# First batch row by token tiles with zero matmuls in the waits, spikes in two rows, additions in turn: a spike and mixture-of-experts layer on one core

## The chip, the core and the metric

The kernel runs on one core of a Trainium2 chip. The core has five engines with queues of their own: TensorE (PE, matmuls and transposes into PSUM; its weight loads are listed as PEld), VectorE (DVE), ScalarE (ACT), GpSimd (POOL) and SyncE (SP, which here only issues DMAs; ACT and POOL issue some too). Each engine takes its instructions in the order of its queue, and waits for others through semaphores. The metric is the device time of one execution in microseconds (us). Lines such as L536 are lines of the kernel before.

## The reference

The input `x` is 16 rows of 256 tokens with 256 features, `cond` is 16 x 256, all float32. Two layers are each added to their input:

```python
# layer 0: spikes
rates = relu(x) * 0.001
c = cond[:, None, :] + cumsum(rates, axis=1)          # along the tokens
spikes = floor(c) - previous token's floor(c)         # floor(cond) ahead of token 0
x = x + spikes / 0.001
# layer 1: one shared expert and 2 of 8 routed experts
shared = (silu(x @ w1) * (x @ w3)) @ w2               # 256 -> 512 -> 256
s = sigmoid(concat(x, cond) @ router_W)               # 8 scores for each token
top 2 of s + router_bias; gates = their s, divided by their sum
routed = sum over the 2 of gate * gelu(x @ W1e[e]) @ W2e[e]   # 256 -> 256 -> 256
x = x + (shared + routed) / 3
```

## The kernel before

**Chunks.** The 4096 tokens are cut into 8 chunks of 512, that is two batch rows each. A chunk's `x` is loaded token by partition (`xn`), turned by PE (`turn`, L275) so that features lie on partitions and tokens along the free axis, and goes through the spikes:

- `rate` (ACT, L282) makes relu(x) * 0.001, `keep_x` (ACT, L291) keeps the turned x.
- `scan` (DVE, L306) is a running sum that starts again every 16 tokens (the tile `keep` holds 1, and 0 at each start); `sums` (L316 to L321) copies the last value of each stretch into `tot`, scans those, and adds the result to the stretches.
- `start` (ACT, L334) adds `cond` as a bias, `whole` (ACT, L343) converts to whole numbers, `floor` (DVE, L358 and L359) corrects rounding upwards, `spikes` (L370) subtracts the previous token's floor, `add` (L378) makes x1 = 1000 * spikes + x. The first column of `fl`, the floor of `cond`, is a small copy (L348).

The pieces of work are called `(first row, end, first feature half, end)`. Chunks 1 to 7 do each step on the whole chunk, 128 x 1024 elements (`elementwise`); chunk 0 does its first batch row in two halves by features, then its second row.

**Routing** (`route`): `pl` are the logits (L426), `lt` and `pn` turn them, `ex` is ACT's exp (L442); then some thirteen small DVE operations (L444 to L470) find the first and the second choice and give `hot`, which PE counts per expert (`pr`, L475 to L480). PE turns x1 back (`px`, L496), the place of each copy of a token is worked out (L502 to L509, `at_i`), and POOL scatters the rows to a list per expert in DRAM, `xs` (L513).

**Shared expert.** `shared_hidden` multiplies by w1 and w3 into three PSUM banks `ph` (L536), ACT takes Silu (L546), DVE the product `hs` (L547). `shared_out` multiplies by w2 into two PSUM banks `acc` (L563), DVE adds a third of it to x1 (L574). `all_shared` is one long generator of these pieces, and `unit(n)` takes n of them (1 is one of a chunk's four hidden parts, or half its output) at the place where it is called: this is how PE is kept at work beside everything else.

**Routed experts.** The weights of all experts lie in `we`, loaded in quarters (`load_experts`). `run_blocks` goes through up to 71 blocks of 128 rows of one expert: load from `xs`, DVE transposes, two matmuls (L859, L881) with Gelu between, scatter to `ys` (L890).

**End.** `combine` loads the two results of each token from `ys` in 16 pairs of 128-token tiles (`fetch`) and adds them, times the gate, to what is there (L996, four additions to a pair); a tile's last part to be done starts its store (L589). Pairs and the last shared units alternate.

**What sets the order.** Python emits one stream. Inside `tc.manual_schedule(engines=...)` the named engines keep the order as written; this holds for the start (L614 to L662: PE, ACT, DVE), for everything from the last chunk's routing through the blocks (L710), and for DVE at the end (L1007). Elsewhere, in the loop over chunks above all, a planner orders each queue by its own costs among what is ready, earlier text first; it may also move later work forward into gaps of a written order. SP and POOL are planned everywhere. All of it is fixed when the kernel is built.

Of the kernel before, what the change touches and what calls it, by code (L numbers as in the profile page):

```python
# [13 lines left out]
F32 = mybir.dt.float32  # L14
BF16 = mybir.dt.bfloat16
I32 = mybir.dt.int32
# [22 lines left out]
def kernel(  # L39
# [71 lines left out]
    def load_x(i, pieces=1):  # L111
        xn = xin.tile([P, J, D], F32, tag="xn", name=f"xn_{i}")
        src = xf[ts(i, N), :].rearrange("(j p) d -> p j d", p=P)
        for h in range(pieces):
            js = ts(h, J // pieces)
            nc.sync.dma_start(out=xn[:, js], in_=src[:, js])
        return xn


    xns = {0: load_x(0, NB)}  # L120
    cond_n = const.tile([B, D], F32)
    nc.scalar.dma_start(out=cond_n, in_=cond)
    rw = const.tile([P, 2 * KD, 32], F32)
    nc.vector.memset(rw, 0.0)
    nc.scalar.dma_start(
        out=rw[:, :, :E], in_=router_w.rearrange("(k p) e -> p k e", p=P)
    )
    rb = const.tile([P, E], F32)
    nc.scalar.dma_start(out=rb, in_=router_b.partition_broadcast(P))
# [5 lines left out]
    xns[1] = load_x(1)  # L135
    nc.sync.dma_start(out=w2_sb, in_=w2.rearrange("(s p) d -> p s d", p=P))
# [4 lines left out]
    def load_experts(g):  # L141

        for k in range(KD):
            nc.sync.dma_start(
                out=we_v[ts(g, Q), :, k],
                in_=w1e[:, (g * KD + k) * Q :][:, :Q, :].rearrange("e f h -> f e h"),
            )
        es = ts(g, 2)
        for k in range(KH):
            nc.sync.dma_start(  # L150
                out=we_v[:, es, KD + k], in_=w2e[es, ts(k, P), :].rearrange("e p d -> p e d")
            )
# [7 lines left out]
    keep = const.tile([P, KD * N], F32)  # L160
# [51 lines left out]
    def turn_cond():  # L212
        pc = p_t.tile([P, KD, B], F32, tag="pt", name="pc")
        for k in range(KD):
            nc.tensor.transpose(pc[:, k, :], cond_n[:, ts(k, P)], ident[:B, :B])
        nc.scalar.copy(cond_t, pc)
# [3 lines left out]
    def cond_floor():  # L220
        whole = const.tile([P, KD, B], I32, name="whole")
        nc.gpsimd.tensor_copy(whole, cond_t)
        nc.vector.tensor_tensor(cond_fl, whole, cond_t, ALU.is_gt)
        nc.vector.tensor_tensor(cond_fl, whole, cond_fl, ALU.subtract)
# [18 lines left out]
    class Spikes:  # L243
# [5 lines left out]

        def __init__(self, i):  # L250
            def tile(tag, dt=F32, last=T, pool=tmp):
                return pool.tile([P, NB, KD, last], dt, tag=tag, name=f"{tag}_{i}")

            self.i, self.tile, self.xn = i, tile, xns.pop(i)
            self.xt = prep.tile([P, KD, N], F32, tag="xt", name=f"xt_{i}")
            self.rates = tile("rates")

        @staticmethod
        def cut(t, part):

            b, bb, k, kk = part
            if bb - b == 1:
                return t[:, b, k:kk, :].rearrange("p k t -> p (k t)")
            return t[:, b:bb, k:kk, :].rearrange("p b k t -> p (b k t)")
# [32 lines left out]
        def scan_tiles(self):  # L297
            self.seg = self.tile("tb")
            self.tot, self.base = self.tile("tot", last=NSEG), self.tile("base", last=NSEG)
            self.cs, self.ri = self.tile("ta"), self.tile("tc", I32)  # L300
            nc.vector.memset(self.tot[:, :, :, 0:1], 0.0)

        def scan(self, part):

            seg = self.cut(self.seg, part)
            nc.vector.tensor_tensor_scan(  # L306
                seg, keep[:, : seg.shape[1]], self.cut(self.rates, part), 0.0, ALU.mult, ALU.add
            )

        def sums(self, part):  # L310

            seg, tot, base, cs = (
                self.cut(t, part) for t in (self.seg, self.tot, self.base, self.cs)
            )
            n = tot.shape[1]
            nc.vector.tensor_copy(  # L316
                tot.rearrange("p (g s) -> p g s", s=NSEG)[:, :, 1:],
                seg.rearrange("p (g s q) -> p g s q", s=NSEG, q=SEG)[:, :, : NSEG - 1, SEG - 1],
            )
            nc.vector.tensor_tensor_scan(base, keep[:, :n], tot, 0.0, ALU.mult, ALU.add)  # L320
            nc.vector.tensor_tensor(  # L321
                cs.rearrange("p (s q) -> p s q", q=SEG),
                seg.rearrange("p (s q) -> p s q", q=SEG),
                base[:, :, None].to_broadcast([P, n, SEG]),
                ALU.add,
            )
# [18 lines left out]
        def floor_tiles(self, pool=tmp, tag="tb", eng=nc.vector):  # L345

            self.fl = self.tile(tag, last=W, pool=pool)
            eng.tensor_copy(  # L348
                self.fl[:, :, :, 0].rearrange("p b k -> p k b"), cond_fl[:, :, ts(self.i, NB)]
            )  # L350
            self.x1 = x1s[self.i] = keepp.tile(
                [P, KD, N], F32, tag="x1", name=f"x1_{self.i}", bufs=6
            )

        def floor(self, part):

            up, ri = self.cut(self.cs, part), self.cut(self.ri, part)
            nc.vector.tensor_tensor(up, ri, up, ALU.is_gt)  # L358
            nc.vector.tensor_tensor(  # L359
                self.cut(self.fl, part).rearrange("p (g t) -> p g t", t=W)[:, :, 1:],  # L360
                ri.rearrange("p (g t) -> p g t", t=T),
                up.rearrange("p (g t) -> p g t", t=T),
                ALU.subtract,
            )
# [16 lines left out]

    def elementwise(i, sp=None):

        if sp is None:
            sp = Spikes(i)
            for k in range(KD):
                half = (0, NB, k, k + 1)
                pt = sp.turn(half)
                sp.rate(half, pt)
                sp.keep_x(half, pt)  # L390
            sp.next_load()
            yield
        part = (0, NB, 0, KD)
        sp.scan_tiles()
        sp.scan(part)
        yield
        sp.sums(part)
        yield
        sp.start(part)
        sp.whole(part)  # L400
        yield
        sp.floor_tiles()
        sp.floor(part)
        yield
        sp.spikes(part)
        yield
        sp.add(part)
        yield
# [4 lines left out]
    def route(i):  # L413
        x1, x1t = x1s[i], x1ts[i]

        def small(tag, shape=(P, J, E), dt=F32):
            return rt.tile(list(shape), dt, tag=tag, name=f"{tag}_{i}")
# [47 lines left out]
        )  # L465
        sel2 = small("sel2")
# [37 lines left out]
        at = small("at", (P, TOPK, J))  # L504
        for q in range(TOPK):
            nc.vector.tensor_tensor(mine[:, q], row, hots[q], ALU.mult)
        nc.vector.tensor_reduce(at, mine, AX.X, ALU.add)
        at_i = small("at_i", (P, TOPK, J), I32)
        placed[i] = nc.vector.tensor_copy(at_i, at)  # L509
# [84 lines left out]
    def all_shared():  # L594

        for i in range(NCHUNK):
            yield from shared_hidden(i, [slice(0, T), slice(T, N)] if i == 0 else [slice(0, N)])
            if i > 0:
                yield from shared_out(i - 1)
        yield from shared_out(NCHUNK - 1)  # L600
# [12 lines left out]

    with tc.manual_schedule(engines={PE, ACT, DVE}):  # L614
        sp = Spikes(0)
        halves = [(0, 1, k, k + 1) for k in range(KD)]
        row = (1, 2, 0, KD)
        pts = [sp.turn(part) for part in halves]
        for part, pt in zip(halves, pts):
            sp.rate(part, pt)  # L620
        turn_cond()
        for part, pt in zip(halves, pts):
            sp.keep_x(part, pt)
        sp.scan_tiles()
        for part in halves:
            sp.scan(part)
            sp.sums(part)
            sp.start(part)
            sp.whole(part)
        cond_floor()  # L630
        sp.floor_tiles(pool=hid, tag="ht", eng=nc.gpsimd)
        pt = sp.turn(row)
        sp.rate(row, pt)
        sp.keep_x(row, pt)
        sp.next_load()
        for part in halves:
            sp.floor(part)
            sp.spikes(part)
            sp.add(part)
        unit(0.5, whole=False)  # L640
        sp.scan(row)
        sp.sums(row)
        unit(0.5, whole=False)
        sp.start(row)
        unit(0.5, whole=False)
# [7 lines left out]
        unit(0.5, whole=False)  # L653
# [18 lines left out]
    next(ro)  # L672
    unit(0.5)
    next(ro)
    next(ro)
    next(ro)
    next(ro)
    next(el)
    unit(0.5)
    next(el)  # L680
# [4 lines left out]
    for i in range(2, NCHUNK):  # L685
# [9 lines left out]
        next(ro)  # L695
        unit()
# [6 lines left out]
        next(el, None)  # L703
# [10 lines left out]
    unit(0.5)  # L714
    next(ro)
# [270 lines left out]
    def combine():  # L986
        for n in range(SLOTS):
            fetch(n)
        for n, (i, h) in enumerate(pairs):
            yc = ycs.pop(n)  # L990
            for j in range(2):
                t = i * J + 2 * h + j
                last = x1ts[i][:, 2 * h + j, :, :FQ]
                for q in range(TOPK):
                    y = yc[:, j, TOPK - 1 - q]
                    nc.vector.scalar_tensor_tensor(  # L996
                        y, y, gates[:, q, t : t + 1], last, ALU.mult, ALU.add
                    )
                    last = y
# [55 lines left out]
```

## Time and profile before

| | |
|---|---|
| median of 3 runs | 337.07 us (336.89 to 337.3) |
| profiled execution | 337.38 us, of which the span of the core's instructions is 335.7 |
| PE busy in the span | 317.2 us (94%) |
| DVE, ACT, POOL busy | 231.5, 137.9, 165.6 us |
| first matmul of the shared expert | at 10.21 us |
| PE waits for `hot` between 46 and 132 us | 2.9 us in 5 times |
| blocks of routed experts end, last stage begins | about 285.4 us |
| DMA | 50.34 MB, mean 150 GB/s, 364 to 408 GB/s in the slices from about 293 to 319 us |

All times in the text count from the start of the span. A group's line gives its source line, engine and operation, output and inputs, shape and count, then busy time and the mean of one in ns. In a timeline a line begins with start and length in us, and in brackets the engine's idle time before it with what ended it. A wait's line gives who waited for whom, us in total, times, and the longest. Matmuls overlap, so a PE that is shown as busy can be slower than it could be: starts one after another tell the pace.

### The profile page before, as it was taken

Reading aid. Unit: us, or ns where it says so; the run is one execution under the profiler, and the core shown is the slowest. Engines: PE = TensorE matmul, PEld = TensorE weight load, DVE = VectorE, ACT = ScalarE, POOL = GpSimd, SP = SyncE. Lnnn points to the kernel's source line nnn. Section 1 sums busy time; section 2 is a strip of 40 time slices with the busy share of each in tenths; the row PEclk is TensorE's granted clock in tenths of the full one; section 3 lists DMA queues with packets and bytes.
Section 4 is the critical chain, followed back from the end, with each engine's and each line's share of the span. In section 5 each row is a group of like instructions: output and inputs, shape, how many; then the busy total and the mean of one; then the engine's idle time right before and its main releaser. Section 6 shows DMA issues by size and latency. Waiting matters only on the chain. (4 is left out here: it accounts for less than half of the span.)

```text
span 335.7 us, 6544 instructions
## 1 busy us (share of the span) xinstructions
PE 317.2 (94%) x1674; PEld 233.9 (70%) x1674; DVE 231.5 (69%) x656; ACT 137.9 (41%) x287; POOL 165.6 (49%) x197
## 2 busy tenths in 40 slices
PE   3799998999989999999999999999999999999985
PEld 2587644547546745746699998999999998474574
DVE  4677979999999996652467655555546551299993
ACT  4547385644675372040244443444444434201100
POOL 7000274787478687662045555555555565123220
PEclk9999999999999999999999999999999999999999
DMA  6999533242222112354456665765666662499913
GB/s 174 255 217 215 146 114 98 88 136 100 79 81 99 65 64 86 109 194 102 73 109 149 155 149 142 165 140 126 156 150 151 157 146 80 164 364 408 397 70 125
DMA packets 62534, 50.34 MB, mean 150 GB/s; under 512 B 42607, under 2 KB 52864, under 8 KB 62497
## 3 DMA queue, kind: packets, MB, share of 16 engines
q1 hardware_dynamic: 42240, 26.19, 32.0%
q0 software_dynamic: 7456, 20.86, 17.0%
q10 hardware_dynamic: 12800, 2.88, 5.0%
q8 instruction: 14, 0.23, 0.3%
q14 instruction: 24, 0.19, 0.2%
HBM read 27.44 MB, written 22.84 MB: 150 GB/s over the span
## 5 line engine op out<-in xcount | busy, mean ns | idle before, releaser
L536 PE MATMUL ph<-x,w_sb 128*128 128x512 f32 (+1 forms) x288 | 119.3, 561 | 4.9 <-DVE x L378 4.2
L890 POOL DMA_INDIRECT ys<-yb,to x67 | 66.2, 988 | 67.0 <-ACT yb L889 56.4
L513 POOL DMA_INDIRECT xs<-x1t,at_i x64 | 78.8, 1232 | 38.8 <-ACT xt L291 18.7
L536 PEld LDWEIGHTS ph<-x,w_sb 128*128 128x128 f32 x288 | 54.2, 196 | 53.5 <-issue 42.0
L859 PEld LDWEIGHTS phe<-xbt,w1e 128*128 128x128 f32 x536 | 70.3, 191 | 4.7 <-ACT hbt L867 0.9
L859 PE MATMUL phe<-xbt,w1e 128*128 128x128 f32 x536 | 70.7, 275 | 0.7 <-DVE xbt L832 0.7
L881 PE MATMUL py<-we,hbt 128*128 x268 | 68.9, 380 | 0.2 <-ACT hbt L867 0.2
L827 DVE COPY w1e<-we 128x512 f32 x67 | 29.1, 435 | 45.3 <-PE phe L859 43.8
L563 PE MATMUL pa<-w_sb,hs 128*128 128x256 f32 x256 | 58.2, 381 | 1.4 <-DVE x1t L574 1.1
L563 PEld LDWEIGHTS pa<-w_sb,hs 128*128 128x128 f32 x256 | 48.0, 190 | 11.1 <-issue 2.8
L881 PEld LDWEIGHTS py<-we,hbt 128*128 128x128 f32 x268 | 45.9, 191 | 3.9 <-ACT hbt L867 0.4
L546 ACT ACTIVATE as<-ph 128x512 f32<-128x512 f32 (+1 forms) x36 | 19.9, 553 | 64.5 <-PE ph L536 51.8
L867 ACT ACTIVATE hbt<-phe 128x256 f32<-128x256 f32 x67 | 25.8, 384 | 45.6 <-PE phe L859 35.2
L547 DVE TENSOR_TENSOR hs<-as,ph 128x512 f32<-128x512 f32 (+1 forms) x36 | 22.4, 623 | 27.5 <-PE ph L536 20.8
L889 ACT COPY yb<-py 128x256 f32<-128x256 f32 x67 | 24.9, 372 | 22.7 <-PE py L881 22.2
L832 DVE STREAM_TRANSPOSE xbt<-xb 128x256 f32<-128x256 f32 x67 | 29.3, 437 | 0.0
L306 DVE TENSOR_TENSOR_SCAN tb<-keep,rates 128x1024 f32<-128x1024 f32 (+2 forms) x10 | 18.8, 1876 | 1.4 <-ACT rates L282 1.3
L497 ACT COPY x1t<-px 128x512 f32<-128x512 f32 x16 | 8.6, 592 | 25.1 <-PE px L496 25.1
L589 POOL DMA_DIRECT2D out_dram<-yc x8 | 5.8, 729 | 23.9 <-DVE yc L996 22.1
L334 ACT ACTIVATE ta<-ta,cond_t 128x256 f32<-128x256 f32 x32 | 14.1, 498 | 8.1 <-DVE ta L321 7.1
L463 POOL COPY x1t<-first 128x16 f32<-128x16 f32 x8 | 4.2, 519 | 23.1 <-DVE first L456 23.1
L574 DVE SCALAR_TENSOR_TENSOR x1t<-pa,x1t 128x512 f32<-128x512 f32 x14 | 9.6, 684 | 6.3 <-PE pa L563 6.3
(135 smaller groups left out, 268.2 us busy)
## 6 DMA issues: line engine op xcount, KB each, us to landing
xb<-xs SPq DMA_DIRECT2D x184, 33.0 KB
yc<-ys SPq DMA_DIRECT2D x8, 512.0 KB
we<-ys SPq DMA_DIRECT2D x8, 512.0 KB
xn<-in_x_dram SPq DMA_DIRECT2D x7, 512.0 KB
xb<-xs ACTq DMA_DIRECT2D x84, 33.0 KB
we<-in_L_cond_W1e_dram SPq DMA_DIRECT2D x8, 256.0 KB
we<-in_L_cond_W2e_dram SPq DMA_DIRECT2D x8, 256.0 KB
out_dram<-yc POOLq DMA_DIRECT2D x8, 256.0 KB, 4.3
```

The source lines that it names most:

```text
L513: nc.gpsimd.indirect_dma_start(out=xs_w[(i * J + j) * TOPK + q][:, :], out_offset=bass.IndirectOffsetOnAxis(ap=at_i[:, q, j : j + 1], axis=0),
L536: nc.tensor.matmul(ph, lhsT=w[:, k, ts(u, P)], rhs=x1[:, k, cols], start=(k == 0), stop=(k == KD - 1),)
L546: nc.scalar.activation(act, ps[0], AF.Silu)
L547: nc.vector.tensor_tensor(ht[:, u, cols], act, ps[1], ALU.mult)
L563: nc.tensor.matmul(pa[:, q, :], lhsT=ht[:, s, ts(n * h + q, P)], rhs=w2_sb[:, s, :], start=(s == 0), stop=(s == KS - 1),)
L827: nc.vector.tensor_copy(w, we[:, bass.ds(off, KD * HE)])
L832: nc.vector.transpose(xt.rearrange("p g k r -> p g (k r)"), block[b].pop("xb")[:, :, :FQ])
L859: nc.tensor.matmul(ph[:, m, :].rearrange("p (g r) -> p g r", r=Q), lhsT=w[:, k, ts(m, P)], rhs=xt[:, :, k, :], start=(k == 0), stop=(k == ...
L867: nc.scalar.activation(ht, ph, AF.Gelu)
L881: nc.tensor.matmul(py, lhsT=ht[:, k, :], rhs=we[:, bass.ds(off + KD * HE + k * D, D)], start=(k == 0), stop=(k == KH - 1),)
L889: nc.scalar.copy(yb, py)
L890: nc.gpsimd.indirect_dma_start(out=ys_w[b][:, :], out_offset=bass.IndirectOffsetOnAxis(ap=to[:, b : b + 1], axis=0), in_=yb, in_offset=Non ...
```

## The change

*First batch row of chunk 0 by token tiles.* A class `FirstRow` handles the row in two tiles of 128 tokens, both feature halves together, instead of two feature halves of 256 tokens. The sums are two small scans, chained from tile to tile; `start` and `whole` become one ACT instruction per feature half (bias and conversion together), and `floor` adds the bias itself. The shared expert's first slice becomes two of 128 tokens. The first x load is in three pieces (128, 128 and 256 tokens).

*Zero matmuls.* `keep_busy(n)` multiplies a tile of bf16 zeros, 128 x 512, into a PSUM bank that nothing reads: five ahead of the transposes of `cond`, three after the row's transposes, five after those of the second row.

*Tables and loads.* A Silu of one column comes first on ACT. `rw` and `rb`, the router's weights and bias, are issued from SP after chunk 1's x and no longer from ACT. The experts' quarters are issued behind a later x load (`issue_after`: queue order on SP). `cond_t` and the floor of `cond` are made on DVE.

*Spikes in two rows.* `elementwise` does chunks 1 to 7 row by row (128 x 512 elements), in another order: the second row's scan, sums and conversions go beside the first's. `sums` no longer copies: the scan reads the last values with a stride, and the addition is in place. The first column of `fl` is copied by ACT. In `route` a new yield stands between the first and the second choice, and the loop puts the first row's floor there. `at_i` is reduced straight into whole numbers, without a cast.

*Additions take turns.* In `combine` both tiles of a pair get their first expert's result, then both the second's.

```diff
+    def load_x(i, pieces=(J,)):
 ...
+        for n in pieces:
+            x_loads[i] = nc.sync.dma_start(out=xn[:, j : j + n], in_=src[:, j : j + n])
+            j += n
...
+    busy = const.tile([P, N], BF16)
+    nc.vector.memset(busy, 0.0)
+    xns = {0: load_x(0, (1, 1, 2))}
...
+    warm = const.tile([P, 1], F32)
+    nc.vector.memset(warm, 0.0)
+    nc.scalar.activation(warm, warm, AF.Silu)
...
     xns[1] = load_x(1)
+    nc.sync.dma_start(
+        out=rw[:, :, :E], in_=router_w.rearrange("(k p) e -> p k e", p=P)
+    )
+    rb = const.tile([P, E], F32)
+    nc.sync.dma_start(out=rb, in_=router_b.partition_broadcast(P))
...
     def load_experts(g):
+        with tc.issue_after(x_loads[g + 3].ins):
+            load_quarter(g)
...
         def sums(self, part):
-            nc.vector.tensor_copy(
-                tot.rearrange("p (g s) -> p g s", s=NSEG)[:, :, 1:],
-                seg.rearrange("p (g s q) -> p g s q", s=NSEG, q=SEG)[:, :, : NSEG - 1, SEG - 1],
-            )
-            nc.vector.tensor_tensor_scan(base, keep[:, :n], tot, 0.0, ALU.mult, ALU.add)
...
+            nc.vector.tensor_tensor_scan(
+                upto, keep[:, :n], cs[:, :, SEG - 1], 0.0, ALU.mult, ALU.add
+            )
...
+    class FirstRow:
+        def whole(self, j):
+            cs, ri = self.halves(j)
+            for k in range(KD):
+                nc.scalar.activation(ri[:, k], cs[:, k], AF.Identity, bias=cond_t[:, k, 0:1])
+
+        def floor(self, j):
+            cs, ri = self.halves(j)
+            for k in range(KD):
+                nc.vector.scalar_tensor_tensor(
+                    cs[:, k], cs[:, k], cond_t[:, k, 0:1], ri[:, k], ALU.add, ALU.is_lt
+                )
+            nc.vector.tensor_tensor(
+                self.sp.fl[:, 0, :, j * P + 1 : (j + 1) * P + 1], ri, cs, ALU.subtract
+            )
...
     def elementwise(i, sp=None):
+        one, two = [(b, b + 1, 0, KD) for b in range(NB)]
...
+        sp.scan(one)
+        yield
+        sp.sums(one)
+        sp.start(one)
+        sp.whole(one)
+        sp.scan(two)
+        yield
+        sp.sums(two)
+        sp.start(two)
+        sp.whole(two)
         sp.floor_tiles()
+        yield
+        sp.floor(one)
+        yield
+        sp.spikes(one)
+        sp.add(one)
+        sp.floor(two)
+        yield
+        sp.spikes(two)
+        sp.add(two)
         yield
...
             x1t[:, :, :, FQ + 1], key_first[:, :, None].to_broadcast([P, J, NQ])
         )
+        yield
         sel2 = small("sel2")
...
+    def keep_busy(n):
+        for _ in range(n):
+            nc.tensor.matmul(idle, lhsT=busy[:, :P], rhs=busy, start=True, stop=True)
+
     with tc.manual_schedule(engines={PE, ACT, DVE}):
         sp = Spikes(0)
+        one = FirstRow(sp)
+        keep_busy(5)
         turn_cond()
+        cond_floor()
+        pts = [one.turn(j) for j in range(2)]
+        keep_busy(3)
+        one.rate(0, pts[0])
+        one.keep_x(0, pts[0])
+        one.rate(1, pts[1])
         sp.scan_tiles()
+        sp.floor_tiles(copy=nc.gpsimd.tensor_copy)
+        one.scan(0)
+        one.sums(0)
+        one.whole(0)
+        one.keep_x(1, pts[1])
+        one.scan(1)
         pt = sp.turn(row)
         sp.rate(row, pt)
+        sp.next_load()
+        keep_busy(5)
+        one.floor(0)
+        one.spikes(0)
+        one.add(0)
+        one.sums(1)
+        one.whole(1)
         sp.keep_x(row, pt)
+        sp.scan((1, 2, 0, 1))
+        unit(0.25)
+        one.floor(1)
+        unit(0.25)
+        one.spikes(1)
+        unit(0.25)
+        one.add(1)
+        unit(0.25)
+        sp.scan((1, 2, 1, 2))
+        unit(0.25, whole=False)
         sp.sums(row)
...
         next(ro)
         next(el, None)
         next(ro)
+        next(el, None)
+        next(ro)
         unit()
...
-            for j in range(2):
-                t = i * J + 2 * h + j
-                last = x1ts[i][:, 2 * h + j, :, :FQ]
-                for q in range(TOPK):
+            last = [x1ts[i][:, 2 * h + j, :, :FQ] for j in range(2)]
+            for q in range(TOPK):
+                for j in range(2):
+                    t = i * J + 2 * h + j
                     y = yc[:, j, TOPK - 1 - q]
                     nc.vector.scalar_tensor_tensor(
-                        y, y, gates[:, q, t : t + 1], last, ALU.mult, ALU.add
+                        y, y, gates[:, q, t : t + 1], last[j], ALU.mult, ALU.add
                     )
-                    last = y
+                    last[j] = y
```

## The prediction

> **What bounds the kernel now.** I read the busy times first, then busy time by stretch, the timelines of TensorE (PE) and VectorE (DVE), and the waits.
>
> ```profile
> PE 317.2 (94%) x1674; PEld 233.9 (70%) x1674; DVE 231.5 (69%) x656; ACT 137.9 (41%) x287; POOL 165.6 (49%) x197
> ...
> 3.60:10.20 6.60, 2.53 (x10) 1.72 (x10) 5.00 (x15) 4.54 (x13) 3.32 (x14) 1.00 0.84 257
> 10.20:16.20 6.00, 5.49 (x12) 3.97 (x13) 4.23 (x9) 2.38 (x4) 0.00 (x0) 1.00 1.14 220
> 16.20:46.00 29.80, 29.46 (x174) 21.21 (x174) 22.51 (x56) 16.50 (x31) 5.74 (x5) 1.00 0.85 181
> 46.00:132.00 86.00, 82.37 (x388) 46.14 (x386) 81.63 (x222) 50.30 (x89) 62.04 (x52) 1.00 0.27 91
> 285.40:335.70 50.30, 45.55 (x152) 28.63 (x152) 36.65 (x79) 5.46 (x8) 11.28 (x16) 1.00 0.68 255
> ```
>
> Columns: stretch, length, busy us of PE, weight loads, DVE, ACT and POOL, then the granted clock. From 10.2 us on PE hardly stops: the end is PE's start, plus its fixed work, plus what it loses. It loses in three places.
>
> ```profile
> 10.21 1.22 PE L536 MATMUL ph<-x,w_sb 128*128 128x256 f32 x2 [3.75 <-DVE x L378]
> 11.93 4.92 PE L536 MATMUL ph<-x,w_sb 128*128 128x256 f32 x12 [0.50 <-DVE x L378]
> ...
> L536 PE MATMUL ph<-x,w_sb x13: 379/379/487, 15.9 to 18.6; 128*128 128x256 f32 x13
> ```
>
> The start: PE waits for spikes until 10.21, for their second half until 11.93, and until 16.2 its matmuls start 0.427 us apart, afterwards 0.216. The granted clock says 1.00 throughout; only the pace shows it. By 16.25 PE had issued 12 matmuls, 2.6 us of work at full pace, so it stands where a PE at full pace from 13.65 would.
>
> ```profile
> PE pr L475 <- DVE hot L470: 2.9, 5, 0.9
> PE pl L426 <- ACT as L546: 0.5, 1, 0.5
> PE pl L426 <- DVE at_i L509: 0.2, 1, 0.2
> ...
> 49.71 1.22 DVE L358 TENSOR_TENSOR ta<-tc,ta 128x1024 f32<-128x1024 int32 x1
> 50.85 0.18 DVE L458 TENSOR_TENSOR chosen<-key,second 128x32 f32<-128x32 f32 x1
> 50.96 1.24 DVE L359 TENSOR_TENSOR tb<-tc,ta 128x1024 f32<-128x1024 int32 x1
> 52.13 0.18 DVE L470 TENSOR_TENSOR hot<-chosen,chosen 128x32 bf16<-128x32 f32 x1
> ```
>
> The middle (46 to 132 us, DVE as full as PE): PE waits 3.6 us, mostly for `hot`, whose 0.19 us operations queue behind 1.2 us pieces of the next chunk's floor.
>
> ```profile
> 293.83 0.48 DVE L996 SCALAR_TENSOR_TENSOR yc<-yc,gates 128x256 f32<-128x256 f32 x1
> 294.23 0.48 DVE L996 SCALAR_TENSOR_TENSOR yc<-yc,gates,x1t 128x256 f32<-128x256 f32 x1
> 294.75 0.48 DVE L996 SCALAR_TENSOR_TENSOR yc<-yc,gates 128x256 f32<-128x256 f32 x1
> ...
> 326.45 1.99 PE L563 MATMUL pa<-w_sb,hs 128*128 128x256 f32 x8 [1.15 <-DVE x1t L574]
> 328.74 3.72 PE L563 MATMUL pa<-w_sb,hs 128*128 128x256 f32 x16 [0.30 <-DVE we L574]
> ```
>
> The tail: from 292.7 to 328.6 DVE runs without a break, and PE waits twice for a PSUM bank that a DVE addition (L574), late behind the combination, frees.
>
> **The change, part by part.**
>
> *First row by token tiles.* The new path, from the old rows. The first x piece, now half as large, has landed by the old 3.66. PE first has five zero matmuls: from about 1.2 (the old first DVE memset ends at 1.1) at 0.427, to 3.4; the transposes of `cond`, 0.4, to 3.8; two transposes of 0.21 and their end, 4.45. Relu 0.40: 4.9. Scan of 256 elements 0.78 (L306): 5.65. Two scans of 8, priced as those of 16 (0.19, overlapping): 5.95. Addition 0.42: 6.4. Two ACT conversions with bias, 128x128: no row; L334 takes 0.50 for 256, `ex` 0.20 for 32; I take 0.40, 0.30 apart: 7.15. DVE scans tile 1 meanwhile. Floor: two comparisons of 128x128, between 0.19 (32) and 0.42 (256), 0.29: 7.5; subtraction, spikes, addition 0.43 each, with gaps: 8.85. PE starts at 8.9.
>
> Then 32 matmuls per tile at 0.109 (the pace of 128-column transposes at 18.84). Two stops follow. Silu's first call queues on ACT behind tile 1's conversions and row 2's `keep_x` (0.58), to about 11; `ph` has three banks, so PE stops some 0.8. And row 2's chain (second scan 0.69, sums 0.23 + 0.66, bias 2 x 0.5, conversion 0.61, floor 2 x 0.69, spikes 0.68, addition 0.69, with the tile's products between) ends near 22, hardly before the old 22.6. Until then PE has both tiles (7.0), chunk 1's transposes (0.9) and the output matmuls of row 1 (16 x 0.216 = 3.5, which the planner can pull forward as it already did with four): 8.9 + 0.8 + 7.0 + 0.9 + 3.5 = 21.1, so a stop of about 1.2. Full-pace start: 8.9 + 0.8 + 1.2 = 10.9. **Gain 13.65 - 10.9 = 2.75**; 4.7 without the stops, 0.8 with twice as much.
>
> *Zero matmuls.* That PE is at full pace at 8.9 is the unproven part. The row: 4.0 us of matmuls in a row (from 11.93) raised the pace. The Trainium skill, "TensorE: Matmul & The Clock Gate", Part 1, calls this a clock gate and asks for a busy window of about 3.4 us to open it; its Part 4 holds that transposes don't count as busy. With transposes, the queue is full from 1.2 to about 6, and the five at the end leave under 3 us idle before 8.9. By Part 4 no window is full (2.1 us, then 1.3, then 2.1), and up to 3.4 us run at half pace: 1.7 us dearer. I take the row; the rule goes into the range.
>
> *Moved tables and loads.* Silu's table (1.28 us at 10.01) is now loaded while x is on its way. Before, PE's slow matmuls hid it (first Silu 13.19); left there it would now cost about 0.7. No gain, no loss. x in three pieces is one more SP issue (0.45) ahead of `w1` and `w3`; x, `w1` and `w3` are 1.5 MB, at 255 GB/s from about 2 us on landed near 8, wanted from 8.9 on: hidden, with 1 us to spare. `rw` and `rb` are issued on SP behind chunk 1's x, two issues of about 0.5, so `w2` goes out about 1.5 later; it had until 20.58, now about 12. 2.5 MB lie ahead at 255 GB/s, landing about 11: nothing, or 1 us if late. The 16 expert loads (0.3 to 0.5 us of SP each) queue behind later x loads; the last now go out after the load of chunk 6's x, at 67.9 in the old trace, and are wanted from 160 on. `cond`'s copy and floor go to DVE, three operations of 0.2 while it waits for Relu. The bank of the zeros is free long before its second user.
>
> *Spikes by rows* (chunks 1 to 7). DVE per chunk before: 2.29 + 0.20 + 0.27 + 1.22 + 0.06 + 0.17 + 1.22 + 1.22 + 4 x 0.68 = 9.4. After: 2 x 1.22 + 2 x 0.23 + 2 x 0.66 + 4 x 0.69 + 4 x 0.68 = 9.7. The choices lose the cast `at_i` (0.16). Net +0.15, 1.0 in seven chunks, dearer. ACT gets 0.37 more per chunk, in idle time (50 of 86 us busy). Against that: no piece in front of a choice is longer than 0.69 (scans 1.22). `hot` took 4.1 to 6.6 us from its first operation; both floor pieces (2.45) lay within it in three chunks; now the first row's two (1.38) are written between the choices and the rest behind. PE's 3.6 us can at most vanish; they can grow by the 1.0 and by 1.2 in each of the chunks that had no floor there. I take **1.3**, a good third.
>
> *Additions take turns.* Independent steps start 0.40 apart, dependent ones 0.515. Of 64 additions 32 change: 32 x 0.115 = 3.7 us less DVE. "VectorE: DVE Perf Modes", Rules for kernel authors, says that chained operations drain the pipe anyway and only their count matters: gain 0. The rows above disagree, and I go by them. Worth is not 3.7 but what PE lost: 1.31 + 0.10 + 0.46 + 0.10 (excess of start-to-start over 0.216 at 326.45 and 328.74, with restarts) = 2.0; then PE is the bound. **Gain 1.9.** The loads of `ys`, issued from 288.8 on, bring 512 KB every 1.3 us (364 to 408 GB/s), while a pair's additions take 1.8 now and 1.6 then: still hidden.
>
> **Sum.** 2.75 + 1.3 + 1.9 = 5.95. The profiled execution took 337.38 (span 335.7, 1.7 around it), so 331.4; the median of the runs is 0.3 lower, so **331.1**.
>
> **Rivals.**
> - *More comes through* (0.17): the stops fill and the waits for `hot` vanish: 4.7 + 3.0 + 1.9 = 9.6, 327.5. For: PE has ready work nearly always; against: row 2's chain.
> - *The gate stays shut at first* (0.12): 1.7 less, 332.8; with the second stop longer, 333.5.
> - *DVE eats the lead* (0.08): it is full from 46 on and gets 1.0 more; then only the tail stays: 337.07 - 1.9 = 335.2. Against: from 16.2 to 46 it is busy 22.5 of 29.8 us, so its backlog can begin earlier too.
> - *Slower* (0.04): `hot` later. The floor between the choices delays each of seven second choices by 1.2 us beyond today: 8.4 - 2.75 - 1.9 = +3.75, 340.8. It decides once the delay passes 0.75 us per chunk. Against: in three chunks more floor lies there already.
> - *No change* (0.03): PE's lead is lost and the last output transfers, not DVE, hold the tail: 337.1. Against: the last PE matmul to the end is one addition and one 128 KB store.
>
> **How the numbers follow.** The forecast keeps 0.56; its own range is 329 to 333.4 (gate partly, `hot` 0 to 2.5). 327.5 to 335.3 leaves out half of the first rival below, and above the far half of the third and the two that gain nothing (some 0.2 in all). 0.2% (0.7 us) is about what a measurement can tell: slower 0.04, same 0.03, faster 0.93.
>
> **What would show it.** Right: the first L536-like matmul near 8.9 with starts 0.109 apart; a short PE stop near 10.5 and one near 21.5; L996 starts all 0.40 apart and no PE wait for L574 after 320; PE waits for `hot` of 2 to 3 us. Wrong: starts 0.21 apart at 9 us (gate); PE waits for `hot` above 5; DVE still unbroken to the last addition.

## The result, and the profile after

The changed kernel takes 334.25 us (median of 6 runs, 333.85 to 334.61), the kernel before, run beside it, 337.0 (336.25 to 337.92): a ratio of 0.9913, 95% interval 0.9898 to 0.9928, or 2.9 us less (2.4 to 3.4). The forecast was 5.95 us less. The profiled execution took 334.24 us, its span is 332.5.

Busy times of the changed kernel, then busy time by stretch with the columns of the same view before; the last stretch begins, as before, with the last hidden stage (285.40 before):

```profile
PE 317.8 (96%) x1719; PEld 234.3 (70%) x1719; DVE 227.3 (68%) x671; ACT 143.7 (43%) x308; POOL 156.1 (47%) x196
...
3.60:10.20 6.60, 4.89 (x28) 3.32 (x29) 5.91 (x19) 2.79 (x9) 2.10 (x11) 1.00 0.95 307
10.20:16.20 6.00, 5.49 (x44) 4.97 (x43) 4.43 (x14) 2.28 (x8) 0.00 (x0) 1.00 0.45 157
16.20:46.00 29.80, 29.50 (x175) 20.11 (x175) 23.90 (x63) 19.25 (x40) 7.09 (x8) 1.00 0.46 122
46.00:132.00 86.00, 80.15 (x397) 45.31 (x398) 78.40 (x225) 55.34 (x100) 56.09 (x52) 1.00 0.38 119
284.40:332.50 48.10, 45.00 (x152) 28.75 (x152) 34.05 (x79) 5.46 (x8) 11.16 (x16) 1.00 0.70 266
```

Between 46 and 132 us PE is busy 2.2 us less than before (80.15 against 82.37), the opposite of what was forecast for that stretch. The last stage is 2.2 us shorter (48.1 against 50.3).

The start, on PE's timeline of the changed kernel:

```profile
4.74 0.89 PE L725 MATMUL idle<-busy 128*128 128x512 bf16 x3
...
9.06 1.60 PE L642 MATMUL ph<-x,w_sb 128*128 128x128 f32 x12 [1.23 <-DVE x L478]
11.18 2.01 PE L642 MATMUL ph<-x,w_sb 128*128 128x128 f32 x14 [0.51 <-ACT as L652]
```

The first hidden matmul stands at 9.06 (forecast 8.9). Twelve of them take 1.60 us and not the 2.7 or so that they would need at half pace, so PE is at full pace at once. One short stop for Silu follows at 11.18 (forecast 10.5, 0.8 us). The second stop that was forecast, near 21.5, is not there: the second row's x1 is complete at 22.0, and PE comes to it at 22.05 without a wait.

PE's waits from 46 to 132 us in the changed kernel (total, times, longest):

```profile
PE ph L642 <- ACT as L652: 2.9, 3, 1.3
PE pr L582 <- DVE hot L577: 1.7, 4, 0.7
PE pn L544 <- DVE tot L326: 1.2, 4, 0.3
PE pt L288 <- DVE row L609: 0.3, 1, 0.3
```

The waits for `hot` fell from 2.9 to 1.7. But 4.4 us of waits are there that were not: for Silu (`as`), for the turned logits (`pn`), for the transposes of the next chunk. Before, all waits in this stretch came to 3.6; now they come to 6.1.

The tail, DVE's and then PE's timeline of the changed kernel:

```profile
291.63 0.69 DVE L653 TENSOR_TENSOR hs<-as,ph 128x512 f32<-128x512 f32 x1 [2.75 <-PE ph L642]
292.23 0.87 DVE L1124 SCALAR_TENSOR_TENSOR yc<-yc,gates,x1t 128x256 f32<-128x256 f32 x2
293.02 0.87 DVE L1124 SCALAR_TENSOR_TENSOR yc<-yc,gates 128x256 f32<-128x256 f32 x2
293.82 0.87 DVE L1124 SCALAR_TENSOR_TENSOR yc<-yc,gates,x1t 128x256 f32<-128x256 f32 x2
...
317.80 11.60 PE L669 MATMUL pa<-w_sb,hs 128*128 128x256 f32 x53
```

Pairs of additions start 0.79 to 0.80 apart (0.40 each), and PE's last 53 matmuls run without a wait: both stops of before are gone.

**Where the time went.** I count the work that PE has behind it at an instant, each matmul of the computation at its full-pace price (0.216 us per 256 float32 columns, zero matmuls at nothing). The lead is that count less the same count in the trace of the kernel before. It moves in steps of a matmul, some 0.2 to 0.4 us, and each lead in this text is that of one profiled execution.

| at, us | 22 | 46 | 85 | 115 | 125 | 145 | 280 | 328 |
|---|---|---|---|---|---|---|---|---|
| changed kernel | 3.0 | 3.4 | 3.4 | 3.0 | 1.1 | 1.3 | 1.1 | 2.6 |

So the start gives 3.0 us, which are kept until 115 us; 1.9 are lost within ten microseconds in chunk 7; the tail adds 1.5 by 328 (the last matmul ends 3.06 earlier than before). The question is what happens at 115 to 125. ACT's timeline there and PE's wait, in the changed kernel, then ACT's at the same place in the kernel before:

```profile
114.28 1.28 ACT L548 ACT_TABLE_LOAD   x1
115.58 0.20 ACT L548 ACTIVATE ex<-pn 128x32 f32<-128x32 f32 x1
116.14 1.33 ACT L341 ACTIVATE tb<-tb,cond_t 128x256 f32<-128x256 f32 x3 [0.37 <-DVE tb L331]
117.38 0.60 ACT L350 CAST tc<-tb 128x512 int32<-128x512 f32 x1
117.89 0.50 ACT L341 ACTIVATE tb<-tb,cond_t 128x256 f32<-128x256 f32 x1
118.41 1.28 ACT L652 ACT_TABLE_LOAD   x1
119.70 0.60 ACT L652 ACTIVATE as<-ph 128x512 f32<-128x512 f32 x1
...
120.35 1.12 PE L642 MATMUL ph<-x,w_sb 128*128 128x512 f32 x2 [1.31 <-ACT as L652]
```

```profile
117.46 0.20 ACT L442 ACTIVATE ex<-pn 128x32 f32<-128x32 f32 x1 [0.40 <-PE pn L438]
117.67 1.28 ACT L546 ACT_TABLE_LOAD   x1
118.97 0.60 ACT L546 ACTIVATE as<-ph 128x512 f32<-128x512 f32 x1
120.85 1.70 ACT L334 ACTIVATE ta<-ta,cond_t 128x256 f32<-128x256 f32 x4 [1.28 <-DVE ta L321]
```

In the changed kernel all four biases of the chunk and the first row's conversion stand between `ex` and the Silu that PE waits for: 4.1 us from `ex` to Silu. Before, the same place held only the table load, 1.5 us, and the biases came after the Silu. My theory from here on: the new middle costs time by ACT's order. The rival from the prediction: DVE, full and with more work, eats the lead.

### The profile page after: what moved, and what is told of

Its sections match the earlier page's. It is cut to its first block, busy times and chain, and to the rows that moved or that the text cites. A ratio compares the mean times of both kernels' runs of the same rounds, so it can differ in the third digit from the quotient of the medians.

```text
span 332.5 us, 6671 instructions
## 1 busy us (share of the span) xinstructions
PE 317.8 (96%) x1719; PEld 234.3 (70%) x1719; DVE 227.3 (68%) x671; ACT 143.7 (43%) x308; POOL 156.1 (47%) x196
## 5 line engine op out<-in xcount | busy, mean ns | idle before, releaser
L642 PE MATMUL ph<-x,w_sb 128*128 128x512 f32 (+2 forms) x320 | 118.1, 514 | 5.4 <-ACT as L652 3.4
L619 POOL DMA_INDIRECT xs<-x1t,at_i x64 | 70.2, 1098 | 44.0 <-issue 16.2
L669 PEld LDWEIGHTS pa<-w_sb,hs 128*128 128x128 f32 x256 | 48.0, 190 | 10.4 <-issue 4.4
L652 ACT ACTIVATE as<-ph 128x512 f32<-128x512 f32 (+2 forms) x40 | 20.3, 513 | 57.5 <-PE ph L642 54.6
L653 DVE TENSOR_TENSOR hs<-as,ph 128x512 f32<-128x512 f32 (+2 forms) x40 | 22.9, 573 | 29.2 <-PE ph L642 23.3
L317 DVE TENSOR_TENSOR_SCAN tb<-keep,rates 128x512 f32<-128x512 f32 (+1 forms) x16 | 18.4, 1148 | 3.6 <-ACT rates L295 3.4
L341 ACT ACTIVATE tb<-tb,cond_t 128x256 f32<-128x256 f32 x30 | 13.9, 502 | 6.1 <-DVE tb L331 6.1
```

The lines of the kernel that those rows point to most:

```text
L619: nc.gpsimd.indirect_dma_start(out=xs_w[(i * J + j) * TOPK + q][:, :], out_offset=bass.IndirectOffsetOnAxis(ap=at_i[:, q, j : j + 1], axis=0),
L642: nc.tensor.matmul(ph, lhsT=w[:, k, ts(u, P)], rhs=x1[:, k, cols], start=(k == 0), stop=(k == KD - 1),)
L652: nc.scalar.activation(act, ps[0], AF.Silu)
L653: nc.vector.tensor_tensor(ht[:, u, cols], act, ps[1], ALU.mult)
L669: nc.tensor.matmul(pa[:, q, :], lhsT=ht[:, s, ts(n * h + q, P)], rhs=w2_sb[:, s, :], start=(s == 0), stop=(s == KS - 1),)
```

## The experiments

Ratios are against the kernel before, run on the same chip beside each (its medians were 337.5, 337.4 and 337.1 in the three groups); "us" behind a ratio is that ratio of 337.2. Some of the expectations count a wait as the excess of one start over the pace, which is a little more than the idle time of the views (1.28 and 1.47 us there are 1.12 and 1.31 here).

**Each part by itself: turns_alone, middle_alone, start_and_turns.** The first is the kernel before with the changed `combine`; the second the kernel before with the new `sums`, `floor_tiles`, `elementwise`, `route` and loop; the third the changed kernel with the old ones for chunks 1 to 7.

```diff
 # turns_alone: kernel before
-            for j in range(2):
-                ...
-                for q in range(TOPK):
+            for q in range(TOPK):
+                for j in range(2):
 # start_and_turns: changed kernel
+    class Whole(Spikes):      # cut, scan_tiles, sums, floor_tiles, floor of the kernel before
-            sp = Spikes(i)
+            sp = Whole(i)     # elementwise, route and the loop: those of before
```

> The kernel before with nothing but the additions of the combination taken in turn (both tiles' first, then both tiles' second). The step of the prediction says a gain of 1.9 us, 335.1 against 337.0, with starts 0.40 apart, and no wait of PE for a shared addition after 320. The rule that chained operations drain anyway says 0: 337.0. If the additions were hidden by the loads of ys, also 337.0.

> The kernel before with the new middle alone: spikes of chunks 1 to 7 in two rows, the new sums, the pause between first and second choice, at_i without a cast; start and combination are the old ones. The prediction's step said a gain of 1.3 us (335.7). Theory now (order on ScalarE: in two chunks a Silu that TensorE needs stands behind the second row's biases and conversions): no gain, 337.0 to 339, with TensorE waits for Silu of 0.5 to 1.5 us that the kernel before does not have. Rival (DVE is full and got more work): 1.0 us of added DVE work, 338.0, with the waits for hot and x, not for Silu.

> The changed kernel with the old middle: chunks 1 to 7 whole, old sums, choices in one piece, old order in the loop; new start and additions in turn stay. Theory (the new middle costs the lead, by ScalarE's order): the start's 3.0 us of lead and the tail's 2.0 both reach the end, 337.0 - 5.0 = 332.0, 2.2 below the changed kernel. Rival (DVE, full from 46 us on in both middles, eats any lead): only the tail stays beside a little, 334.5 to 335.2. Rival (the start gave less than it seems): also about 334, but then the lead is missing at 40 us already.

Measured: turns_alone 335.48, ratio 0.9944 (0.9925 to 0.9962), 1.9 us less. middle_alone 338.7, 1.0044 (1.0027 to 1.0061), 1.5 us more. start_and_turns 334.03, 0.9907 (0.9888 to 0.9927), 3.1 us less.

The tail is worth what was forecast: in turns_alone too PE's last matmuls run without a wait, and the gain of 0 that the prediction read out of the rule on chained operations is ruled out. The new middle alone makes the kernel slower. But start_and_turns does not reach 332, and lies between the theory and its rivals: of the start's lead only about 1.2 us (3.1 less 1.9) reach the end beside the old middle. The lead was 3.0 at 22 us, so the start did give it; it was 2.1 at 46, 1.5 at 85 and 1.3 at 145. PE's waits in start_and_turns from 20 to 132 us:

```profile
PE pr L637 <- DVE hot L632: 2.0, 3, 1.2
PE pa L725 <- DVE hs L709: 0.7, 1, 0.7
PE pn L600 <- DVE tot L511: 0.6, 1, 0.6
PE pl L588 <- ACT as L708: 0.5, 1, 0.5
PE pl L588 <- DVE at_i L671: 0.2, 1, 0.2
```

The last two stand in the kernel before as well; the waits for `hs` and `pn` are new, and both are for DVE. And chunk 7's x1 is complete at 130.6 us there, at 130.8 in the kernel before: although chunk 1's was 1.7 us earlier (37.6 against 39.3), nearly all of that is gone by then, on a DVE that is busy 69.6 of the 72 us from 46 to 118. In the old middle the traces speak for the rival; no run took work from DVE there to show it. In the new one chunk 7's x1 is complete at 126.2, and PE asks for it at 130.5: there DVE is not what the end of the middle waits for.

**The order on ACT: second_row_later, middle_later.** The same edit, once to the changed kernel and once to middle_alone.

```diff
         sp.sums(two)
-        sp.start(two)
-        sp.whole(two)
         sp.floor_tiles()
         yield
         sp.floor(one)
         yield
+        sp.start(two)
+        sp.whole(two)
+        yield
 ...
         unit()
+        next(el, None)
         next(ro)
```

> The changed kernel with the second row's biases and conversion (start and whole) written behind the shared unit that follows the choices, and no longer ahead of it. In ScalarE's queue this puts the first Silu after exp ahead of the second row's two biases in chunk 2 and ahead of two of them in chunk 7, and changes next to nothing else on TensorE. Theory (order on ScalarE): TensorE's waits for Silu of 1.28 us at 46.9 and 1.47 us at 120.4 shrink to under 0.5; at least the second one reaches the end: 332.3 to 332.9, a gain of 1.4 to 1.9 on the changed kernel. Rival (DVE eats the lead): the wait goes over to hot or to x, 334.2 as the changed kernel.

> middle_alone with the second row's biases and conversion behind the shared unit, the same edit as in second_row_later. In ScalarE's queue only chunks 2 and 7 change. Theory (the new middle costs time because of ScalarE's order there): of the 1.2 us that middle_alone is slower than the kernel before, all or more comes back: 336.9 to 337.5 against 338.7. Rival (the 1.0 us of added VectorE work is the cause): 338.2 to 338.7.

Measured: second_row_later 332.61, ratio 0.9865 (0.9843 to 0.9887), 1.6 us below the changed kernel, with intervals that don't overlap, and the lowest ratio of this study. middle_later 337.09, 0.9998 (0.9982 to 1.0015): all that middle_alone lost has come back. PE's waits for Silu from 46 to 132 us, in middle_alone and in middle_later:

```profile
PE ph L532 <- ACT as L542: 2.4, 2, 1.3
PE ph L533 <- ACT as L543: 0.7, 1, 0.7
```

ACT's timeline of second_row_later at the same place:

```profile
115.96 0.20 ACT L549 ACTIVATE ex<-pn 128x32 f32<-128x32 f32 x1
116.53 0.91 ACT L341 ACTIVATE tb<-tb,cond_t 128x256 f32<-128x256 f32 x2 [0.37 <-DVE tb L331]
117.45 1.28 ACT L653 ACT_TABLE_LOAD   x1
118.75 0.60 ACT L653 ACTIVATE as<-ph 128x512 f32<-128x512 f32 x1
119.24 0.61 ACT L350 CAST tc<-tb 128x512 int32<-128x512 f32 x1
119.75 0.91 ACT L341 ACTIVATE tb<-tb,cond_t 128x256 f32<-128x256 f32 x2
```

Two biases and the conversion stand behind the Silu now, which comes 2.8 us after `ex`; PE doesn't wait for it, and the lead is 2.4 at 125 and 2.1 at 145, where the changed kernel had 1.1 and 1.3. The same work on the same engines, in another order at two places of ACT's queue, is worth 1.6 us. DVE's order changes with it at these two places, and two of PE's output matmuls move; POOL's order stays. In chunk 2 PE's wait only fell from 1.12 to 0.75. No loss of middle_alone is left for the rival's 1.0 us of DVE work to explain, though the forecast's gain isn't there either.

**The start: no_zeros, no_zeros_later, no_warm.** The changed kernel without `busy`, `idle` and the three `keep_busy`; the same for second_row_later; the changed kernel without the three lines of `warm`.

> The changed kernel without the thirteen zero matmuls and the memset of their operand. Theory (the pace of TensorE): the first hidden matmuls start 0.21 apart and not 0.109 until some 4 us of them have run, and the lead on the kernel before at 22 us falls from 3.0 to about 1.3 (1.7 less). Since the wait for Silu in chunk 7 leaves only about 1.1 of the lead, hardly any of this reaches the end: 334.2 to 334.7. Rival (any lead of the start reaches the end): 335.9. Rival (the zero matmuls do nothing, other matmuls set the pace): starts 0.109 apart at 9 us, 334.2.

> The kernel second_row_later without the zero matmuls. There the lead reaches the end (2.4 at 145 us). Theory: of the 1.7 us that the slow pace costs, 1.2 to 1.7 show at the end: 333.8 to 334.3 against 332.6. Rival (the zero matmuls do nothing): 332.6. With no_zeros beside it, which should lose 0.5 at most, the pair shows whether chunk 7 levels the lead in the changed kernel.

> The changed kernel without the early Silu: its table is loaded in front of the first Silu, behind chunk 0's conversions. The prediction's step priced this at 0.7 us at the start (the stop of TensorE near 11 us grows from 0.7 to about 1.4 or 2). At the end next to nothing of it shows if chunk 7 levels the lead: 334.2 to 334.7.

Measured: no_zeros 334.82, 0.9933 (0.991 to 0.9955), 0.7 us above the changed kernel, though the intervals overlap. no_zeros_later 333.53, 0.9892 (0.9866 to 0.9917), 0.9 above second_row_later, overlapping too. no_warm 335.33, 0.9960 (0.9945 to 0.9974), 1.6 above the changed kernel, apart from it.

The pace, by form, of the first hidden matmuls: no_zeros from 8.5 to 12.8 us, then the changed kernel from 9 to 12.5.

```profile
L640 PE MATMUL ph<-x,w_sb 128*128 128x128 f32 x19 | 4.4, 429 | 2.1 <-DVE x L476 2.1
```

```profile
L642 PE MATMUL ph<-x,w_sb 128*128 128x128 f32 x23 | 3.1, 284 | 1.7 <-DVE x L478 1.2 <-ACT as L652 0.5
```

Without the zeros the matmuls start 0.213 apart until 12.8 us: the zeros do what the prediction supposed. But they are worth less than its 1.7 us. In no_zeros the first hidden matmul comes 0.48 earlier (8.58; x's transposes needn't queue behind five zero matmuls), and the stop for Silu at 11.2 is gone, since slow matmuls arrive when Silu is done anyway. The lead at 22 us is 2.1, only 0.9 smaller. In the profiled executions of the second pair even that does not show: no_zeros_later is 0.2 us further ahead at 22 us than second_row_later, because its pace doubles near 11.7 already, and because second_row_later waits 0.71 us for a weight load at 10.48.

Silu's table is worth more than the 0.7 it was priced at: in no_warm PE waits 1.92 us for the first Silu and not 0.51, and the lead at 22 us is 1.7. My expectation that chunk 7 levels every lead was wrong: no_warm's wait there stays 1.32, because the whole pipeline, ACT too, shifts with the start, and the loss goes through to the end.

**The choices: choices_unbroken, lt_first.** choices_unbroken holds the first row's floor back until `hot` is made. lt_first starts from second_row_later and holds the first row's scan back until the logits' addition. In both the loop takes its pieces in an order that fits (not shown).

```diff
 # choices_unbroken: changed kernel
+        hot_op[0] = nc.vector.tensor_tensor(hot, hots[0], hots[1], ALU.add)
 ...
-        sp.floor(one)
+        with tc.issue_after(hot_op[0].ins):
+            sp.floor(one)
 # lt_first: second_row_later; lt_op[0] is the logits' addition lt
-        sp.scan(one)
+        with tc.issue_after(lt_op[0].ins) if lt_op[0] else nullcontext():
+            sp.scan(one)
```

> The changed kernel with the first row's floor forced behind hot on VectorE, so that both choices run through. Theory (the chunk's chain on VectorE is what PE follows, the choices are only a part of it): hot comes earlier and TensorE's waits for hot (2.4 us in the changed kernel) fall below 1.5, but x1 of the next chunk comes 1 to 1.4 us later in each chunk and TensorE waits for that: 334 to 336, no gain. Rival (the waits for hot are what is lost, as the prediction's middle step had it): 332 to 333.

> second_row_later with the logits' addition lt forced ahead of the first row's scan on VectorE (the scan takes 1.22 us and TensorE's transpose pn waits 0.45 us behind it in four chunks). Theory (these waits are real losses and VectorE has a little room): up to 4 x 0.45 less, 331.2 to 332.0. Rival (VectorE is full, the scan's delay comes back as a later x1 or hot): 332.6 or more.

Measured: choices_unbroken 333.51, 0.9891 (0.9869 to 0.9913), 0.7 us below the changed kernel with overlapping intervals; lt_first 333.59, 0.9885 (0.9857 to 0.9912), not told apart from second_row_later. Both re-plan all queues, so neither isolates its step. In choices_unbroken PE's waits for `hot` are no smaller (2.2 us from 46 to 132, five times), chunk 7's x1 comes at 130.0 and not at 126.2, and the Silu wait of chunk 7 is not there: neither theory's story. Nothing here says that the floor between the choices made `hot` late. lt_first is 5.4 us ahead at 115 us, without a wait for `pn`, and then loses 4.1 of it in chunk 7: a wait of 2.24 us for Silu, and slow matmuls behind it.

**Silu first everywhere: lt_silu, later_silu.** lt_first and second_row_later, with the second row's biases held behind the last Silu written before them.

```diff
+                silu[0] = nc.scalar.activation(act, ps[0], AF.Silu)
 ...
-        sp.start(two)
+        with tc.issue_after(silu[0].ins):
+            sp.start(two)
```

> lt_first with the second row's biases held behind the last Silu written before them. In lt_first TensorE was 5.4 us ahead of the kernel before at 115 us and lost 4.1 of it in chunk 7, in one wait for Silu of 2.4 us and in matmuls 0.43 apart after it. Theory (ScalarE's order in chunk 7 alone): with the Silu ahead of the biases there, 3 to 4 us of lead reach the end: 330.3 to 331.5. Rival (x1 of chunk 7 or the routing, on VectorE, is then late by as much): 332.5 to 333.5.

> second_row_later with the second row's biases held behind the last Silu written before them, in every chunk. Theory (Silu order): the waits for Silu of 0.91 at 46.4 and 0.64 at 62.9 go too, 332.0 to 332.6. Rival (what Silu gains, the next chunk's x1 loses, since its biases come later): 332.6 to 333.2.

Measured: lt_silu 337.34, 1.0008 (0.9996 to 1.0021); later_silu 332.84, 0.9881 (0.986 to 0.9903), the same as second_row_later within the measurement. The two largest waits of PE in lt_silu from 46 to 132 us:

```profile
PE pr L589 <- DVE hot L584: 4.7, 5, 1.9
PE pl L539 <- DVE x L383: 2.2, 1, 2.2
```

The rival holds, and more: 5.2 us of lead at 125 were shared matmuls done ahead of time. With the biases late in every chunk, chunk 7's x1 is complete only at 131.8, and everything behind it (the routing of the last chunk, the counts, the blocks) waits. By 140 us some 7 us of lead are lost; about 2 of them are PE's clock, which runs at half from 129.5 to 136.3 (last section). A lead of PE counts only as far as the chunk's chain keeps up.

## Why the prediction was right and wrong, point by point

- *Start, 2.75: right, in part by luck.* The lead is 3.0 us at 22 us, with the first of the two stops it named. The second, 1.2 us, did not come: PE was still at work when the second row was ready, because it started 0.16 later and each restart, also after the short stops for a bank, cost it about 0.1 (a first start-to-start of 0.21 instead of 0.11). And the term was added as if every lead reached the end. Beside the old middle about 1.2 of it does (start_and_turns), where DVE is full; the prediction had this as a rival with 0.08 and an end of 335.2.
- *Zero matmuls: right in kind, too dear.* Matmuls start 0.111 apart at 9 us with them, 0.213 without; 0.9 us of lead and 0.7 to 0.9 at the end (not told apart from nothing) instead of 1.7, since the slow pace covers the stop that follows. The moment at which the pace doubles is not fixed by the program: with the same thirteen zero matmuls it lies between 4.74 and 5.04 us in the changed kernel and between 7.31 and 7.55 in second_row_later. On the rule that transposes don't count as busy (the Trainium skill, "TensorE: Matmul & The Clock Gate", Part 4): in the changed kernel the pace doubles some 3.5 us after the first zero matmul, and zero matmuls fill only 2.3 of these, transposes nearly all the rest. That speaks for taking the row; a window that need only be partly full would explain it too, and no run tells the two apart.
- *Silu's table:* that the early load is hidden was right; the "about 0.7" for leaving it where it was is too cheap. It costs 1.4 us more of wait, and 1.6 at the end (no_warm).
- *Moved loads: hidden, but barely.* There is no wait in the changed kernel; in the profiled executions of second_row_later and later_silu PE waited 0.71 and 0.55 us for a weight load (`w3`, by its place) near 10.4, so the margin of 1 us was less than the spread of its landing.
- *Middle, 1.3: the step that failed.* The waits for `hot` fell even further than forecast, from 2.9 to 1.7 where 2 to 3 were expected. What failed is the sentence that ACT's added work lies "in idle time (50 of 86 us busy)", by which the prediction put ACT's part in the middle at nothing. ACT had the time, but its queue did not have the order. In chunks 2 and 7 the first row's conversion and the second row's biases (in chunk 7 the first row's as well) stand between exp and the Silu that frees PE's next PSUM bank, together 2.4 us of PE waits. In place of +1.3 the stretch gave about -2 (lead 3.4 at 46, 1.3 at 145). Behind another unit the same operations give back 1.6 us, with the start (second_row_later) and without it (middle_later).
- *Additions in turn, 1.9: right,* 1.9 measured alone, and both of PE's stops are gone. The gain of 0 that the prediction drew from the rule for chained operations (the Trainium skill, "VectorE: DVE Perf Modes", Rules for kernel authors: "Minimize op *count*, not sems") does not come out here: same count, same operations, 1.9 us.
- *The sum.* 3.0 at 22 us, about -2 in the middle and 1.5 to 2 in the tail make the 2.9 measured. Of the 3.1 us that the forecast was too low, ACT's order at two places accounts for 1.6, shown by undoing it with the start and without it. The rest lies by the trace among the waits for `pn` (1.2 us, behind the first row's scan on DVE), the Silu waits of chunks 2 and 3 that stay (1.2 us) and some 0.3 in the first block; removing these by themselves without a new plan was not tried, and their shares stay open.

## What to carry to other kernels

When work is added to an engine that is half idle, look up what stands behind it in that engine's queue, not how full the engine is: here two biases and a conversion too many in front of one Silu, and two biases in front of another, cost 1.6 us on an engine that was busy 55.3 of 86 us. A lead won at the start is worth what the slowest chain behind it lets through (about 1.2 of 3.0 us beside the old middle), so gains of a start and of a middle need not add; measure them together and apart. And a lead made of deferrable work (5.4 us in lt_first) is no lead if the chain that the end depends on has not moved.

## What the runs showed of the hardware

The slow pace can come back in the middle of a kernel, although PE has been at work for over 100 us. In lt_first PE waited 2.24 us, until 122.69; for about 4 us after that, matmuls of 512 columns started 0.853 us apart and not 0.429. In lt_silu it waited 1.93 us, until 127.76, and 2.20 us, until 131.85. Here the granted clock, the column behind POOL's, shows the change; first lt_first, then lt_silu:

```profile
120.00:122.70 2.70, 0.46 (x3) 0.01 (x1) 2.56 (x9) 2.67 (x5) 2.21 (x2) 1.00 0.28 100
122.70:126.60 3.90, 3.90 (x5) 1.63 (x6) 2.52 (x9) 0.94 (x2) 2.64 (x4) 0.56 0.28 101
126.60:130.00 3.40, 3.40 (x20) 2.07 (x19) 3.26 (x12) 1.01 (x2) 0.00 (x0) 1.00 0.01 4
```

```profile
125.80:127.70 1.90, 0.03 (x1) 0.00 (x0) 1.90 (x7) 0.00 (x0) 1.59 (x2) 1.00 0.29 105
127.70:129.50 1.80, 1.50 (x17) 1.12 (x17) 1.80 (x5) 0.93 (x2) 1.38 (x2) 0.99 0.31 115
129.50:131.80 2.30, 0.15 (x4) 0.00 (x0) 2.30 (x8) 1.43 (x2) 0.00 (x0) 0.50 0.00 0
131.80:136.20 4.40, 4.35 (x20) 3.30 (x21) 0.47 (x2) 0.00 (x0) 2.80 (x3) 0.50 0.17 61
```

In lt_first the five slow matmuls cost 1.8 us, so that this wait cost PE nearly twice its length. In lt_silu the clock was at half before the wait of 2.20 us began: the change came at about 129.5. PE's wait of 1.93 us had then been over for 1.7 us, and PE had mostly worked since, at full pace. In no_warm, after a wait of 1.92 us (until 12.59), the full pace stayed. So the length of one wait does not tell whether the clock falls, and it need not fall in every execution of a kernel: of the six timed runs of lt_first, two list a mean granted clock of 0.995 and 0.994 and four 0.999 or 1.0, while all 22 of lt_silu list 0.984 to 0.99. The Trainium skill ("TensorE: Matmul & The Clock Gate", Part 1) lets the gate close after an idle window of about 3.4 us; in these two executions shorter waits were enough.

At the start of no_zeros (8.58 to 12.80) the clock is given as 1.00 while 19 matmuls run where 38 would fit: before the first full pace only the distance of the starts tells.
